# Layer 0: the dt transfers of the scan steps move from SP's queue to ACT's

## The chip, the core and the metric

The kernel runs on one core of a Trainium2 chip. A core has five engines with an instruction stream each: TensorE (PE, with its weight loads shown as PEld), VectorE (DVE), ScalarE (ACT), GpSimd (POOL) and SyncE (SP). Each engine works through its own stream in order, and streams meet at semaphores. Transfers between device memory and the on-chip memory are run by 16 DMA engines; an instruction on SP, ACT or POOL issues them into a queue of that engine. The metric is the device time of one execution in microseconds. Three executions of the kernel before took 7145.44, 7160.09 and 7180.47 us; the median is 7160.09 us.

## The reference

Four layers follow each other on x of 8 x 128 x 64 x 64, each of the form x + f(group_norm(x)). Layer 0 is a selective scan (a Mamba block) on the first 64 channels and a 3x3 convolution on the other 64; layer 1 passes over rows and columns in four directions, each row adding the relu of a 9-tap convolution of the row before; layer 2 is a product of two convolutions; layer 3 is a deformable convolution with a batch norm. The change lies in the scan of layer 0:

```python
dt = jax.nn.softplus(dbc[..., :R] @ dt_w + dt_b)      # per token, 128 channels
Bm = dbc[..., R:R + N]                                 # per token, N = 16
Cm = dbc[..., R + N:]
A = -jnp.exp(A_log)                                    # 128 channels x 16
dA = jnp.exp(dt[..., None] * A)
dBx = dt[..., None] * Bm[:, :, None, :] * xc[..., None]

def step(h, inp):
    dA_t, dBx_t, C_t = inp
    h = dA_t * h + dBx_t
    return (h, jnp.einsum('bdn,bn->bd', h, C_t))
```

For every image there are 128 x 16 recurrences of 4096 tokens.

## The kernel before, in words

**Tiling of the scan.** An image's 4096 tokens are cut into 4 chunks of 1024, so there are 32 chunks for 8 images; a chunk has two halves of T = 512 tokens. The 128 x 16 recurrences do not fit 128 partitions, so a half is worked off in 8 *steps*, each of 16 channels: a step has two tiles side by side (j = 0, 1), and in each, 8 channels times 16 states fill the 128 partitions. That gives 16 steps a chunk and 512 steps in all (`where`, L584).

**What one step needs.** The chunk's part of the program computes dt and u = dt * xc for 128 channels and stores both to device memory (`v_store`, L449, tiles dtd and ud). A step then reads 8 rows of them back, each repeated for the 16 states. This is `spread` (L590): for each j one transfer of 128 partitions x 512 floats, 256 KB, so two transfers for dt (k = 0) and two for u (k = 1). `step_dt` (L598) brings dt into a tile `da` (5 buffers); `step_u` (L602) brings u into a tile `hb` (6 buffers).

Then the step runs through the engines:

- `step_decay` (L606, ACT): da = exp(a * da) in place, two activations.
- `step_scan` (L612, DVE): ub = hb * B into PSUM (L619), and two hardware scans over 512 tokens (L627) that write the states back into hb. With the scan, da is free again.
- `step_carry` and `step_weigh` (L631, L635, POOL): the last states are kept for the next half; hb = hb * C.
- `round_sum` (L640, PE): for every two steps, four matmuls with a matrix of ones and zeros sum over the states into ps_y. With these, hb is free again.

**The order of the work.** Nothing is reordered by a scheduler: the loop at L659 writes the streams in a fixed order, and this order is the order on each engine and in each queue. Iteration i holds, in this order: step_scan(i); the vector instruction of layer 1 (`layer1.add`); step_dt(i + 4); round_sum(i - 3) if i is odd; step_u(i + 3); step_decay(i + 2); step_carry and step_weigh(i - 1); the events planned for iteration i; the matmuls of layer 1 (`layer1.products`). The events are the chunk's other work, planned by `plan_chunk` (L338) at fixed places relative to the chunk's first step: projections on PE and their evacuation by ACT (L368, L369, L402, L413, L428, L429, L461, L505, L516), Silu (L417) and Ln (`logs`, L300) with their table loads on ACT, the softplus sums on POOL, stores and loads on SP. The evacuated PSUM tiles (`ps_g`) share two buffers, so PE's next projection waits for ACT's evacuation of the one before the last.

**Layer 1 beside it.** From iteration 269 on, half of the images pass through layer 1 while layer 0 goes on: every iteration adds 9 matmuls (L763) and one vector instruction (L771). A new direction of layer 1 loads its weights (L752) on SP just ahead of its first matmuls.

**Transfers and their semaphores.** All transfers of layer 0 are issued by SP. Transfers that SP or ACT issue take eight completion semaphores in turn, in the order of the program, so an issue waits until the transfer eight places earlier has landed.

Of the kernel before, what the change touches and what calls it, by code (L numbers as in the profile page):

```python
# [22 lines left out]
GC, D, DI, N, R, KC = 64, 64, 128, 16, 4, 3  # L23
T = 512
# [140 lines left out]
def layer0(tc, a, ident, gmat, x_in, x1d, mid, norm1, layer1):  # L165
# [5 lines left out]
    nc = tc.nc  # L171
# [4 lines left out]
    with ExitStack() as ctx:  # L176
# [38 lines left out]
        with tc.manual_schedule():  # L215
# [368 lines left out]
            def where(i):  # L584

                return i // 16, i // 8 % 2, i // 2 % 4, 2 * (i % 2)
# [3 lines left out]
            def spread(i, k, t):  # L590

                c, h, r, j0 = where(i)
                for j in (0, 1):
                    d = 32 * (j0 + j) + 8 * r
                    src = dtu[c % 2][h][k][d : d + 8, :]
                    nc.sync.dma_start(t[:, j], src.unsqueeze(0).to_broadcast([N, 8, T]))

            def step_dt(i):  # L598
                steps[i] = {"da": w2.tile([P, 2, T], F32, name="da", bufs=5)}
                spread(i, 0, steps[i]["da"])  # L600

            def step_u(i):  # L602
                steps[i]["hb"] = w2.tile([P, 2, T], F32, name="hb", bufs=6)
                spread(i, 1, steps[i]["hb"])
# [810 lines left out]
```

## Time and profile before

| | |
|---|---|
| median of three runs | 7160.09 us (7145.44 to 7180.47) |
| profiled execution: time | 7110.95 us |
| profiled execution: span, first to last instruction | 7109.2 us |
| layer 0, first to last scan | 87.6 to about 2801 us |
| busy over the span: PE, DVE, ACT, POOL | 71%, 68%, 50%, 57% |
| da transfers on SP | 1024 of 256 KB |
| hb (u) transfers on SP | 1024 of 256 KB |
| moved over the whole span | 1496.93 MB, 211 GB/s on average |

The page gives busy time for each engine, and shares over slices of the span. In a line of a group, the first number after the bar is the busy time in us, then the mean of one instruction in ns, then the idle time of the engine before these instructions with what ended it. "L610 ACT ACTIVATE da<-da,a_neg" is line 610 on ACT, writing tile da from da and a_neg. An engine's name with a q (SPq, ACTq) is its sequencer: issues of transfers and waits, which are not busy time. In the views of waits a line reads: who waited, for whom, how long in total, how often, the longest. PEclk is the clock that TensorE was granted, DMA the mean busy share of the 16 DMA engines.

### The profile page before, as it was taken

What the parts mean: (1) busy time and instruction counts of PE and PEld (TensorE: products, weight loads), DVE (VectorE), ACT (ScalarE), POOL (GpSimd) and SP (SyncE); (2) the same over time, 40 slices, a digit from 0 to 9 for tenths busy, and PEclk for the clock granted to TensorE, in tenths of its full rate; (3) what the DMA queues carried; (4) which work ended last, traced back from release to release, by engine and by line L of the source; (5) the groups of instructions that cost most, each with busy time, mean ns of one, the idle gap of its engine ahead of it and who ended that gap; (6) DMA issues with size and microseconds to landing.
All of it is one profiled execution on the core that took longest, in us unless ns stands there. A gap on an engine that the chain in (4) does not pass through costs nothing. (4 is left out here: it accounts for less than half of the span.)

```text
span 7109.2 us, 74945 instructions
## 1 busy us (share of the span) xinstructions
PE 5077.6 (71%) x21034; PEld 3201.4 (45%) x21034; DVE 4815.8 (68%) x6350; ACT 3530.0 (50%) x8194; POOL 4037.7 (57%) x3739
## 2 busy tenths in 40 slices
PE   4666566799999999699987978975556565564331
PEld 1111111366666666477676766753333333333221
DVE  5988888777777766411466756768667676776667
ACT  4656656544444442200355545554556655655554
POOL 4877777665655554000355556566666666666661
PEclk7666666799999999899999989987767777687665
DMA  6999999988888876501366656677666666667668
GB/s 198 303 284 279 287 302 276 263 224 221 221 217 217 221 207 163 169 20 52 120 189 187 203 174 198 198 222 245 208 208 221 209 210 212 208 207 229 182 181 287
DMA packets 666176, 1496.93 MB, mean 211 GB/s; under 512 B 92712, under 2 KB 127792, under 8 KB 663712
## 3 DMA queue, kind: packets, MB, share of 16 engines
q1 hardware_dynamic: 475680, 871.24, 43.2%
q0 software_dynamic: 184320, 604.13, 27.9%
q10 hardware_dynamic: 5760, 16.78, 0.6%
q8 instruction: 168, 2.75, 0.2%
q14 instruction: 248, 2.03, 0.1%
HBM read 1337.03 MB, written 154.76 MB: 210 GB/s over the span
## 5 line engine op out<-in xcount | busy, mean ns | idle before, releaser
L1213 POOL DMA_INDIRECT X<-table,idx x1386 | 1318.5, 951 | 715.8 <-issue 273.4
L1213 POOL DMA_INDIRECT got<-table,idx x918 | 885.0, 964 | 1204.9 <-DVE idx L1103 508.5
L638 POOL TENSOR_TENSOR hb<-hb,C 128x1024 f32<-128x1024 f32 x512 | 1209.1, 2362 | 40.9
L627 DVE TENSOR_TENSOR_SCAN hb<-da,carry,ps_ub 128x512 f32<-128x512 f32 x896 | 1097.9, 1266 | 55.1 <-DVE ps_ub L619 0.5
L771 DVE SCALAR_TENSOR_TENSOR X<-ps_l,X 128x256 f32<-128x256 f32 x504 | 212.1, 421 | 1138.7 <-PE ps_l L763 954.5
L610 ACT ACTIVATE da<-da,a_neg 128x512 f32<-128x512 f32 x1024 | 695.2, 716 | 545.6 <-DMA da<-dtd 492.4
L1259 ACT COPY samp<-ps_s 128x384 f32<-128x384 f32 x768 | 362.5, 472 | 1039.4 <-remote 625.8
L1224 ACT ACTIVATE X<-X,wgt 128x128 f32<-128x128 f32 x2772 | 863.4, 396 | 9.8 <-issue 9.7
L1267 PE MATMUL ps_o<-samp,dcn_w 128*128 128x256 f32 x2304 | 706.6, 452 | 160.2 <-issue 119.7
L1249 PE MATMUL ps_s<-ident,X 128*128 128x128 f32 x1386 | 305.8, 343 | 595.6 <-ACT samp L1259 282.9
L619 DVE TENSOR_TENSOR ps_ub<-hb,ps_b 128x1024 f32<-128x1024 f32 x512 | 625.7, 1222 | 118.8 <-DMA hb<-ud 113.1
L1267 PEld LDWEIGHTS ps_o<-samp,dcn_w 128*128 128x128 f32 x2304 | 504.3, 230 | 282.6 <-issue 153.4
L646 PE MATMUL ps_y<-hb,m_y 128*32 128x512 f32 x2048 | 413.1, 758 | 269.1 <-DVE y L477 183.2
L1240 DVE TENSOR_TENSOR prod<-prod,X 128x384 f32<-128x384 f32 x462 | 260.9, 565 | 475.0 <-ACT X L1224 310.7
L633 POOL COPY carry<-hb 128x2 f32<-128x2 f32 x512 | 111.9, 219 | 826.6 <-DVE hb L627 789.2
L763 PE MATMUL ps_l<-X,w_left 128*128 128x256 f32 x2268 | 521.2, 386 | 80.6 <-DVE X L771 48.8
L763 PE MATMUL ps_l<-X,w_right 128*128 128x256 f32 x2268 | 524.9, 388 | 69.7 <-DVE X L771 58.3
L1224 ACT ACTIVATE got<-got,wgt 128x128 f32<-128x128 f32 x1836 | 570.4, 393 | 2.4 <-DMA got<-table,idx 2.4
L763 PE MATMUL ps_l<-X,w_up 128*128 128x256 f32 x2268 | 518.3, 384 | 48.3 <-DVE X L771 24.1
L763 PE MATMUL ps_l<-X,w_down 128*128 128x256 f32 x2268 | 516.6, 383 | 35.7 <-DVE X L771 27.3
L1249 PEld LDWEIGHTS ps_s<-ident,X 128*128 128x128 f32 x1386 | 206.1, 176 | 727.1 <-ACT samp L1259 357.6
L763 PEld LDWEIGHTS ps_l<-X,w_right 128*128 128x128 f32 x2268 | 438.7, 197 | 171.3 <-DVE X L771 83.7
(217 smaller groups left out, 8412.0 us busy)
## 6 DMA issues: line engine op xcount, KB each, us to landing
da<-dtd SPq DMA_DIRECT2D x1024, 256.0 KB
hb<-ud SPq DMA_DIRECT2D x1024, 256.0 KB
table<-tok SPq DMA_DIRECT2D x128, 256.0 KB
x<-x1d SPq DMA_DIRECT2D x96, 256.0 KB
X<-table,idx POOLq DMA_INDIRECT x1386
x<-x2d SPq DMA_DIRECT2D x48, 384.0 KB
x3h<-x3d SPq DMA_DIRECT2D x16, 1056.0 KB
x_st<-in_x SPq DMA_DIRECT2D x64, 256.0 KB
```

Source lines behind the costliest of these rows:

```text
L610: nc.scalar.activation(da[:, j], da[:, j], AF.Exp, scale=a_neg[:, r, j0 + j : j0 + j + 1])
L619: nc.vector.tensor_mul(ub, hb, s["B", h].unsqueeze(1).to_broadcast([P, 2, T]))
L627: nc.vector.tensor_tensor_scan(hb[:, j, :], st["da"][:, j, :], ub[:, j, :], start, ALU.mult, ALU.add)
L638: nc.gpsimd.tensor_mul(hb, hb, S[c]["C", h].unsqueeze(1).to_broadcast([P, 2, T]))
L646: nc.tensor.matmul(S[c]["ps_y", h][32 * j : 32 * j + 32, :], lhsT=m_y[:, r, :], rhs=steps[i + j // 2]["hb"][:, j % 2, :], start=(r == 0), ...
L763: nc.tensor.matmul(ps[:, c0:c1, :], lhsT=w[:, k, :], rhs=v[:, prev, c0 + k - PAD : c1 + k - PAD, :], start=(k == PAD), stop=(k == K - 1),)
L1213: nc.gpsimd.indirect_dma_start(out=got[:, k, :, :].rearrange("p q c -> p (q c)"), out_offset=None, in_=tab, in_offset=bass.IndirectOffsetO ...
L1224: nc.scalar.activation(got[:, k, q, :], got[:, k, q, :], AF.Identity, scale=wgt[:, t, k0 + k, q : q + 1])
L1240: nc.vector.tensor_add(prod[:, :, 0, :], prod[:, :, 0, :], got[:, :, 2, :])
L1249: nc.tensor.transpose(ps[:, k, :], got[:, k, 0, :], self.ident)
L1259: self.nc.scalar.copy(self.samp[k0][:, :, col : col + P], ps)
L1267: nc.tensor.matmul(ps, lhsT=self.dcn_w[:, k, :], rhs=samp[:, k - k0, :], start=(k == 0), stop=(k == KK - 1))
```

## The change

In `spread`, the transfers with k = 0 (dt) are issued by ACT instead of SP; those with k = 1 (u) stay on SP. The places of both in the program's order stay as they are, and so do tiles, buffers and sizes.

```diff
                 for j in (0, 1):
                     d = 32 * (j0 + j) + 8 * r
                     src = dtu[c % 2][h][k][d : d + 8, :]
-                    nc.sync.dma_start(t[:, j], src.unsqueeze(0).to_broadcast([N, 8, T]))
+                    queue = nc.sync if k else nc.scalar
+                    queue.dma_start(t[:, j], src.unsqueeze(0).to_broadcast([N, 8, T]))
```

In ACT's stream the two issues of step_dt(i + 4) stand right ahead of the two activations of step_decay(i + 2), behind the events of iteration i - 1. What the issues have to wait for (the buffer of da, the stored dt, the semaphore of the transfer eight places earlier) ACT now waits for, in its own stream. All later line numbers of the file grow by one.

## The prediction

> **What bounds the kernel now.** I read the slices of the page first, since the change touches only layer 0, which ends near 2815 us (its last scan starts at 2798.7 us). Slices are 178 us each; digits are tenths.
>
> ```profile
> PE   4666566799999999699987978975556565564331
> ...
> DVE  5988888777777766411466756768667676776667
> ACT  4656656544444442200355545554556655655554
> ...
> DMA  6999999988888876501366656677666666667668
> ```
>
> Two stages show. Up to about 1400 us DMA stands at 9 and PE at 5 to 7; from there to 2800 us PE stands at 9 and DMA at 7 to 8. In the second stage the matmuls of layer 1 (`products`) run beside the steps of layer 0. The busy time of the two stretches gives the figures.
>
> ```profile
> core 0: us, PE busy (x) PEld busy (x) DVE busy (x) ACT busy (x) POOL busy (x), PEclk, DMA share, GB/s
> 100.00:1360.00 1260.00, 808.02 (x2345) 192.30 (x2346) 1087.44 (x988) 754.83 (x1068) 960.99 (x742) 0.64 1.04 289
> 1440.00:2720.00 1280.00, 1210.53 (x5667) 807.65 (x5666) 933.74 (x967) 553.97 (x806) 752.47 (x585) 0.98 0.82 219
> ```
>
> First stretch: the 16 DMA engines have a share of 1.04 (packets overlap a little), DVE 86%, ACT 60%. From the packet records I counted half-microseconds: in 1.3% of this time the engines lack work. 268 steps pass, 4.7 us each. Second stretch: PE is busy 95% of the time and the engines lack work for a fifth of it; 212 steps, 6.0 us each; a chunk of 16 steps takes 92.4 us, nearly to the tenth, over and over. So the first half is bound by the DMA engines, the second by PE.
>
> Next, what SP itself waits for in its queue, first stretch and second (issuer, releaser: us, times, longest):
>
> ```profile
> SPq L596 <- DMA hb<-ud: 111.5, 272, 0.9
> SPq L596 <- DMA da<-dtd: 92.5, 256, 1.0
> SPq L596 <- PE ps_y L646: 73.8, 46, 5.5
> SPq L596 <- DVE hb L627: 44.3, 70, 2.3
> ```
>
> ```profile
> SPq L596 <- PE ps_y L646: 573.1, 106, 16.3
> ```
>
> The first two lines are the limit on transfers in flight: the program gives its transfers eight completion semaphores in turn, and an issue waits until the transfer eight places earlier has landed. The ps_y lines are u: its buffer hb comes free only after round_sum on PE, and the dt behind it in SP's queue waits too, 573 us in the second stretch.
>
> Last, ACT: a normal chunk in the second half, and an issue from ACT's own queue (only the end of the kernel has them).
>
> ```profile
> 1648.54 1.37 ACT L505 ACTIVATE res<-ps_c,conv_b 64x512 f32<-64x512 f32 x2 [12.09 <-PE ps_c L497]
> 1649.94 1.33 ACT L610 ACTIVATE da<-da,a_neg 128x512 f32<-128x512 f32 x2
> 1655.29 1.26 ACT L402 ACTIVATE xz<-ps_x,b_xc 128x512 f32<-128x512 f32 x2 [4.02 <-issue]
> 1656.45 1.33 ACT L610 ACTIVATE da<-da,a_neg 128x512 f32<-128x512 f32 x2
> 1661.25 1.26 ACT L413 ACTIVATE xz<-ps_z,in_b 128x512 f32<-128x512 f32 x2 [3.47 <-PE ps_z L411]
> ```
>
> ```profile
> 7030.06 1.24 ACT L1348 ACTIVATE X<-X,bn_shift,bn_sc 128x1024 f32<-128x1024 f32 x1 [1.78 <-DVE x3k L1352]
> 7030.14 0.37 ACTq L1353 DMA_DIRECT2D out<-x3k  x1
> 7031.20 1.23 ACT L1348 ACTIVATE X<-X,bn_shift,bn_sc 128x1024 f32<-128x1024 f32 x1
> ```
>
> ACT comes early to what PE makes for it (brackets: 12, 4 and 3.5 us of waiting), and an issue (0.37 us) runs while the activation before it is still computing.
>
> **The change, part by part.** *Issues.* 1024 transfers of 256 KB leave SP and come to ACT, two per step, just ahead of step_decay(i+2). The nearest row is their issue on SP:
>
> ```profile
> L596 SPq DMA_DIRECT2D da<-dtd x1024: 514/526/1790, 76.8 to 2773.7; - x171
> ```
>
> So 1.05 us a step. The issue in the end stage lay under the running activation, and a decay lasts 0.72 us; I let 0.5 us a step show: 0.5 x 512 = 256 us of ACT over the layer. ACT is idle 1260 - 755 = 505 us in the first stretch and 1280 - 554 = 726 us in the second, so it fits. If nothing were hidden it would be 1.05 x 268 = 281 us in the first, which fits too. On the path: 0.
>
> *Waits that come to ACT.* (a) da has five buffers, so dt(i+4) waits for step_scan(i-1) on DVE. Behind it on ACT stand decay(i+2) and all of that iteration's events (evacuations of PSUM, Silu, Ln); PE waits for those, DVE for the decay. Taken step by step from the trace, the scan ends after decay(i+2) starts today in 25% of the steps of the first half and 36% of the second, by 3.6 us at the 95th percentile. (b) The semaphore of eight transfers earlier: by the order of issue that is mostly dt(i+2), which ACT needs next anyway, or u(i+1); some are x_o, x1d or dtd transfers of SP. (c) At a chunk's start, dtd itself. With (a), (b) and the whole 1.05 us together, decay(i+2) would start 1.2 us later on average in the first half and 1.8 in the second; of its lead over the scan that uses it (median 9 and 13.6 us) at least 2.9 us is left at every step. In the second half (a) bites in iterations 10 to 15 of a chunk, ahead of the 12 us wait for ps_c, which swallows it; PE's Silu-fed matmul (L427) starts typically 7 us after Silu. On the path: 0. Between ends: if all of (a) and (b) got through once per chunk, 3.6 us x 32 chunks = +115; below nothing: none, as a wait added to ACT gives nothing back.
>
> *What SP sheds.* dt no longer stands behind u's wait for PE. Today SP issues dt(i+4) later than ACT reaches its place: by 0.9 us (median, first half) and 1.75 us (second). In the second half PE is the bound and decays lead by 9 us and more at 95 steps in 100, so the 573 us are not on the path: 0. In the first half the gain can only be the 1.3% in which the engines lack work: between 0 and -17 us; I take the middle, -8.
>
> *Weights of the next direction.* PE stood idle 9.5, 10.4 and 7.6 us at the three switches inside the layer, waiting for a 576 KB load on SP. It now shares the engines with dt from another queue instead of queueing behind it: half of 27.5 us either way, ±14; I take 0.
>
> *The rate of the engines.* dt and u would now reach the engines from two queues at once, which no row of layer 0 shows. Stretches of 72 us in the first half moved from 262 to 323 GB/s with the same kinds of transfer, so the order in which packets mix does move the rate. Ends: 1260 x (1 - 289/323) = -133 us, and 1260 x (289/262 - 1) = +130. The value taken is 0, as the mean over the stage is a mix already.
>
> A rule speaks against any gain here: the Trainium skill, "DMA: Bandwidth & Descriptors", section "Issuing engines are not separate DMA queues", says that transfers started by different engines run on the same 16 DMA engines and interleave, and that only issue time is saved. By the rule this term is 0; by the fastest stretch above it could be -133; issue time is no bound by SP's rows.
>
> **Sum.** 0 + 0 - 8 + 0 + 0 = -8 us. The profiled execution took 7110.95 us (span 7109.2 and 1.75 around it), 49.1 below the median of the runs, 7160.09. So 7103 in its terms, 7152 as a median.
>
> **The rivals.** *Faster by mixing.* Two queues break the march of 16 engines through the same rows. For it: 262 to 323 GB/s today, and a 2 KB packet took 117 ns on average in the first half, while stores at the same time took 84 to 91 ns. Against: b_in, C and plain loads are as slow, 115 to 130 ns, so the cause may lie elsewhere. Half of the 133: -67, with the -8: 7085.
>
> *Slower: the engines run dry behind ACT.* One mechanism: while ACT is held, no dt is issued. Its longest blocks are Silu (table 1.28, 1.91, table 1.28: 4.5 us) and the Ln group at 873.51 to 878.4 us (4.9), 9.4 us a chunk. If the engines stand still for half, 4.7 x 17 chunks of the first half = +80: 7240. It decides once dt is later than today by more than is in flight: transfers land about 5 us after issue in the first half (from the packet records). Against: ACT's place is 3.1 us behind SP's issue at the 95th percentile, and u still flows.
>
> *Slower by mixing.* The same unknown with the other sign, half of 130: +65, 7217.
>
> **How the numbers follow.** No real change 0.40; faster by mixing 0.33; engines dry 0.17; slower by mixing 0.10. Half a percent, 36 us, is about what this kernel's runs can tell (they span 7145 to 7180). So faster 0.33, same 0.40, slower 0.27. The likeliest case's own range is 7124 to 7196. Cases of both signs are likely, so the 80% range reaches 100 us below 7152, past the middle of the faster case, and 78 above, to where the dry case has begun to bite: 7052 to 7230.
>
> **What the profile after would show.** Right: 1024 da transfers in ACT's queue at about 0.52 us; DMA share still 1.0 and about 4.7 us a step up to 1400 us; 92.4 us a chunk afterwards; SP's ps_y wait still there, now holding u alone. Mixing: the first half's GB/s moves with the share still at 1.0. Dry: the share falls below 1 with ACT waiting for DVE or a landing. The forecast is wrong, too, if the 92.4 us grow, with PE waiting for an activation of ACT.

## The result and the profile after

Four executions of the changed kernel took 7272.43 to 7299.74 us, with a median of 7279.16; four of the kernel before had a median of 7152.76. The ratio is 1.0174, with a 95% interval of 1.0154 to 1.0194: 126 us slower. The profiled execution took 7272.43 us, its span 7270.7. The profiled execution of the kernel before, 7110.95 us, was 42 us under its median, this one 7 under: the two profiles lie 161 us apart, 35 of them behind layer 0, where nothing was changed.

The slices of the page tell where. Changed kernel, 182 us a slice, digits in tenths:

```profile
PE   4555565599998999699898978975556555565331
...
DVE  4778777777677777420376666758667676676667
ACT  4555555554444443210255555554556655555554
...
DMA  6999999988787878410266666667666666667667
```

The first half is lower on DVE and ACT; the digits of DMA hardly show it, since a 9 stands for 90% or more. The two stretches that the prediction used, for the changed kernel:

```profile
core 0: us, PE busy (x) PEld busy (x) DVE busy (x) ACT busy (x) POOL busy (x), PEclk, DMA share, GB/s
100.00:1360.00 1260.00, 722.73 (x2112) 168.68 (x2114) 989.18 (x891) 688.52 (x976) 856.36 (x671) 0.64 0.96 261
1440.00:2720.00 1280.00, 1195.25 (x5531) 788.18 (x5524) 939.72 (x977) 586.45 (x843) 754.79 (x587) 0.97 0.82 222
```

In the first stretch the DMA share fell from 1.04 to 0.96, 289 to 261 GB/s, and every engine does about 9% less work in the same time (DVE 1087 to 989 us, ACT 755 to 689). The second stretch is as it was. For sizes I use one measure throughout, read from the trace: the time from the ub product of step 8 to that of step 264, 256 steps of the first half, below called *the stage*. It took 1197.4 us before and 1321.9 after: +124.5, nearly all that layer 0 lost (126.7 from the first scan to the last). Steps 272 to 448 took 1063.2 and 1060.4, and the usual chunk of the second half takes 92.4 us in both. The loss has two parts. Counted in half-microseconds, the engines lacked work for 1.4% of the stage before and for 8.7% after (17 and 115 us, +98); and a 2 KB packet took 117.0 ns before, 119.1 after, 1.8% or some 20 us more. Each stage is of one profiled execution, so differences of some 10 us between runs carry no weight here.

The issues themselves came out as drawn. The row of ACT's queue for the tile da in the changed kernel, durations as minimum, median and maximum in ns:

```profile
L597 ACTq DMA_DIRECT2D da<-dtd x1024: 521/522/1671, 75.6 to 2899.4; - x171
```

What is new are waits. First ACT's, 100 to 1400 us, before and then after (who waited, for whom, us in total, times, longest):

```profile
ACT da L610 <- DMA da<-dtd: 238.8, 172, 4.4
ACT X L738 <- DMA x<-x1d: 111.7, 32, 8.7
ACT res L505 <- PE ps_c L497: 59.2, 14, 8.5
```

```profile
ACT da L611 <- DMA hb<-ud: 193.1, 61, 7.0
ACT da L611 <- DMA da<-dtd: 83.0, 30, 5.4
ACT da L611 <- DVE ps_ub L620: 67.5, 22, 6.2
ACT da L611 <- DVE hb L628: 54.9, 23, 4.6
```

Before, a decay waited for its own dt: ACT had come early. After, the same place waits for landings of u (193 us) and for DVE (67.5 and 54.9): that is what the issues ahead of the decay wait for, the semaphore of the transfer eight places earlier and the buffer of da. Counted from the records, the decays wait for their own operands only 6 us of the stage now; before it was 253 us. ACT has gone from early to late.

Then DVE's waits in the same time, before and after:

```profile
DVE ps_ub L619 <- DMA hb<-ud: 91.2, 71, 3.2
DVE gm L282 <- PE ps_gn L281: 37.5, 5, 9.0
```

```profile
DVE hb L628 <- ACT da L611: 61.8, 41, 4.5
DVE xz L435 <- ACT xz L432: 58.8, 12, 5.2
DVE gm L282 <- PE ps_gn L281: 51.8, 4, 14.1
DVE ps_ub L620 <- ACT ps_b L473: 37.6, 16, 4.4
DVE ps_ub L620 <- DMA hb<-ud: 20.9, 13, 2.8
```

Before, no wait of DVE for ACT stands above half a microsecond in total; after, there are three, 158 us: scans for decays, `v_round` (L435) for `v_exp` (L432), and the first ub product of a chunk for the copy of B into PSUM (L473). Against that DVE waits 70 us less for u. By position the loss lies there too: over 15 chunks of the first half, the mean time from one ub product to the next grew at steps 3 and 4 of a chunk (+0.9 and +1.2 us), 6 (+3.4), 14 and 15 (+1.3 and +3.2); at 1 and 2 it fell by 0.9 each; the rest is within 0.25. A chunk went from 74.6 to 82.5 us.

One held issue, in the timeline of ACT's stream in the changed kernel (start us, us, engine, line, what; in brackets the idle time before it and what ended it):

```profile
753.63 0.54 ACTq L597 DMA_DIRECT2D da<-dtd  x1
754.00 1.25 ACT L413 ACTIVATE xz<-ps_z,in_b 128x512 f32<-128x512 f32 x2
757.86 0.52 ACTq L597 DMA_DIRECT2D da<-dtd  x1
758.42 1.33 ACT L611 ACTIVATE da<-da,a_neg 128x512 f32<-128x512 f32 x2 [3.18 <-DMA hb<-ud]
762.27 1.18 ACTq L597 DMA_DIRECT2D da<-dtd  x2
763.50 0.72 ACT L611 ACTIVATE da<-da,a_neg 128x512 f32<-128x512 f32 x1 [3.74 <-DMA x_st<-in_x]
```

The first issue of a pair goes at 753.63, the second only at 757.86, when a u transfer has landed; the decay, whose data has long been there, starts 0.56 us later. The next pair is held until 762.27.

SP, which the change was to relieve, waits longer for PE than before: dt no longer stands ahead of u in its queue, and PE runs later behind ACT (from 100 to 1400 us its waits for ACT add up to 331 us, before to 133). SP's queue in the changed kernel, 100 to 1400 us, and then 1440 to 2720:

```profile
SPq L597 <- PE ps_y L647: 454.9, 91, 14.6
```

```profile
SPq L597 <- PE ps_y L647: 748.1, 105, 17.8
```

The first was 85 us before in the same time. The second was 573, and costs nothing: PE bounds that half.

### The profile page after: what moved, and what is told of

Read it like the earlier page. It is cut to its first block, busy times and chain, and to the rows that moved or that the text cites. A ratio compares the mean times of both kernels' runs of the same rounds, so it can differ in the third digit from the quotient of the medians.

```text
span 7270.7 us, 74786 instructions
## 1 busy us (share of the span) xinstructions
PE 5090.7 (70%) x21034; PEld 3209.2 (44%) x21034; DVE 4824.2 (66%) x6350; ACT 3534.6 (49%) x8194; POOL 4017.8 (55%) x3739
## 4 chain that ended last, share of the span: by engine, by line
PE 29%; ACT 11%; another core or an unknown queue 7%; issue 6%; DVE 5%; DMA 2%; POOL 0%; SPq 0%; ACTq 0%; DVEq 0%; POOLq 0%
PE ps_l L764 13%; ACT X L1225 6%; PE ps_o L1268 5%; PE ps_t L926 4%; PE ps_s L1250 3%; PE ps_off L1043 2%; PE ps_t L952 2%; ACT samp L1260 1%; ACT got L1225 1%; DVE prod L1230 1%; DVE X L772 1%; DVE prod L1241 0%; DMA x<-x1d 0%; DVE got L1242 0%
## 5 line engine op out<-in xcount | busy, mean ns | idle before, releaser
L764 PE MATMUL ps_l<-X,w_up 128*128 128x256 f32 x2268 | 517.3, 384 | 54.9 <-DVE X L772 34.5
L764 PEld LDWEIGHTS ps_l<-X,w_left 128*128 128x128 f32 x2268 | 439.9, 198 | 182.1 <-DVE X L772 81.6
```

Source lines behind the costliest of these rows:

```text
L764: nc.tensor.matmul(ps[:, c0:c1, :], lhsT=w[:, k, :], rhs=v[:, prev, c0 + k - PAD : c1 + k - PAD, :], start=(k == PAD), stop=(k == K - 1),)
```

## The experiments

Three theories stood at the start. **The loop** (where an expectation uses letters: L, and L2 in the form through PE): ACT and SP hold each other through the completion semaphores and through u's wait for PE. **Mixing**: two queues make the engines themselves slower. **ACT is full**: issue time, holds and the tie to DVE's scan use up ACT's idle time, so that all that ACT makes comes late. (In the expectations I is the issue time alone, B the tie alone; L3, that a held ACT holds back the next dt.) Layer 0 takes about the same time on the chips used (the stage of the controls h3 and j2: 1203 and 1213 us), but on those of the last seven runs the later layers are faster (the kernel before takes some 6660 us there), so the stage, not the whole time, is compared between calls. Each ratio is against the kernel before on its own chip.

| run | what is on ACT | ratio, 95% interval | stage us | engines lack work |
|---|---|---|---|---|
| before | - | 1 | 1197.4 | 1.4% |
| after | dt | 1.0174 [1.0154, 1.0194] | 1321.9 | 8.7% |
| e1_u_one_act | dt; u as one transfer | 1.0290 [1.0273, 1.0308] | 1398.8 | 9.5% |
| e2_u_one_sp | control: u as one | 1.0150 [1.0131, 1.0169] | 1290.3 | 4.0% |
| e3_act_busy | issue time alone | 1.0014 [1.0003, 1.0024] | 1212.8 | 1.9% |
| e4_act_tie | tie alone | 1.0028 [1.0013, 1.0043] | 1225.8 | 1.8% |
| f1_act_lane | hold alone | 1.0012 [0.9995, 1.0029] | 1201.5 | 2.0% |
| f2_u_later_act | dt; u one iteration later | 1.0200 [1.0174, 1.0226] | 1343.5 | 8.1% |
| f3_u_later_sp | control: u later | 1.0040 [1.0026, 1.0054] | 1243.7 | 3.2% |
| f4_u_on_act | u, with dt on SP | 1.0281 [1.0256, 1.0306] | 1352.9 | 8.3% |
| g1_act_hold | hold and tie | 1.0068 [1.0047, 1.0089] | 1245.2 | 3.2% |
| g2_free_act | dt; u free of PE | 1.0178 [1.0154, 1.0203] | 1340.5 | 8.4% |
| g3_free_sp | control: u free of PE | 0.9944 [0.9926, 0.9963] | 1169.5 | 1.3% |
| h1_act_all | issue time, hold and tie | 1.0141 [1.0109, 1.0173] | 1290.7 | 4.7% |
| h2_short_act | dt; decays cut short | 1.0055 [1.0038, 1.0073] | 1247.0 | 3.0% |
| h3_short_sp | control: decays cut short | 0.9989 [0.9973, 1.0005] | 1203.3 | 1.0% |
| h4_half_act | half of dt | 1.0065 [1.0038, 1.0091] | 1240.3 | 2.2% |
| i1_later_act | dt, behind the decays | 1.0211 [1.0193, 1.0228] | 1338.5 | 7.8% |
| j1_round_act | dt; v_round later | 1.0182 [1.0165, 1.0199] | 1316.3 | 7.6% |
| j2_round_sp | control: v_round later | 1.0027 [1.0012, 1.0043] | 1212.6 | 1.8% |

### Fewer transfers per step, and the burdens one by one

u as one transfer of 512 KB (the two rows of a pair lie side by side in ud, so its store is changed too), with dt on ACT and on SP; a cut of the edit:

```diff
 ...
+                if k:
+                    src = dtu[c % 2][h][k][8 * r : 8 * r + 8, j0 : j0 + 2, :].rearrange("q a t -> q (a t)")
+                    queue.dma_start(t.rearrange("p a t -> p (a t)"), src.unsqueeze(0).to_broadcast([N, 8, 2 * T]))
+                    return
 ...
```

> dt stays on ACT in two issues a step; u becomes one transfer of 512 KB on SP (rows of a pair stored side by side), so that a step takes three completion semaphores of the eight instead of four and the transfer eight places earlier is an older one. Theory L (ACT is held at its issues by the semaphore of the transfer eight places earlier): most of the hold goes, steps 8 to 264 take 1190 to 1250 us instead of 1322, within 40 us of the same kernel with dt on SP. Theory I (the time of the issues on ACT) and theory B (the wait for scan(i-1) on ACT): nothing changes for them, 1300 to 1340 us and 100 to 140 us behind the same kernel with dt on SP.

> The control of the one above: u as one transfer, dt back on SP. All theories: the first half stays bound by the DMA engines, steps 8 to 264 take 1140 to 1210 us (before: 1197); packets of 4 KB may make it somewhat shorter.

Measured: 1398.8 against 1290.3, so dt on ACT costs 108 us with three semaphores a step in place of four. The loop expected at most 40; that failed, and 108 lies in the 100 to 140 of the others. The stages themselves are longer than any expectation, since the control is itself 1.5% slower than the kernel before, where 1140 to 1210 us was expected.

The two other runs leave all transfers on SP and give ACT one burden each at the place of the dt issues: three activations of 128x128 on a scratch tile (issue time), or a write of one column into da(i-1), which waits for the scan of step i-1 and which SP's dt must then wait for (the tie).

```diff
+                    for _ in range(3):
+                        nc.scalar.activation(spare, spare, AF.Identity)
                     step_dt(i + 4)
```

> The kernel before (dt on SP), with three activations of 128x128 on a scratch tile put on ACT where step_dt stands, about 0.9 us of ACT time a step and no wait. Theory I: about the loss of the change, +90 to +130 us. Theories L and B: ACT is idle 40% of the first half, so 0 to +25 us.

```diff
+                    if i >= 1:
+                        nc.scalar.activation(steps[i - 1]["da"][:, 0, 0:1], eps, AF.Identity)
                     step_dt(i + 4)
```

> The kernel before (dt on SP), with an activation of one column into the buffer of da(i-1) put on ACT where step_dt stands: ACT waits there for scan(i-1), and SP's dt(i+4) for that place of ACT, but no issue and no semaphore of another transfer stands on ACT. Theory B: +90 to +130 us. Theories L and I: 0 to +35 us.

Measured: +15 and +28 us of the stage. ACT was busy 76% of the stage in e3 and still had 100 us of decays that came early. Neither alone makes 125.

### The hold, the loop through u, and u on ACT

f1 lets ACT wait, at the same place, for the landing of u(i+1), and do nothing else. f2 and f3 bring u one iteration later, so that it waits less for PE. f4 puts u on ACT and leaves dt on SP. The edits of f1, of f2 and f3, and of f4:

```diff
+                    if i >= 0:
+                        nc.scalar.activation(spare, steps[i + 1]["hb"][:, 1, T - 1 : T], AF.Identity)
                     step_dt(i + 4)
```

> The kernel before (dt and u on SP), with one activation on ACT where step_dt stands that reads one column of hb(i+1) after its transfer: ACT waits for the landing of u(i+1), as the semaphore of the transfer eight places earlier makes it in the changed kernel, but no issue stands on ACT and there is one queue. Theory L2 (a loop: ACT waits for u to land, SP issues u late because it waits for round_sum on PE, and PE waits for ACT's evacuations and Silu): +50 to +130 us, with PE waiting for ACT much longer than before. If this wait is not the cause: 0 to +25 us.

```diff
-                if 0 <= i + 3 < n_steps:
-                    step_u(i + 3)
+                if 0 <= i + 2 < n_steps:
+                    step_u(i + 2)
```

> The changed kernel (dt on ACT) with u issued one step later in the program, step_u(i+2) instead of step_u(i+3): SP then asks for a buffer of hb that PE freed an iteration earlier, so its wait for ps_y shrinks, and the transfer eight places before dt is an older u. Theory L2: most of the loss is gone, within 50 us of the same with dt on SP. If the loss came from issue time, from the wait for scan(i-1) or from mixing two queues: still 90 to 140 us behind the same with dt on SP.

> The control of the one above: the kernel before with step_u(i+2) instead of step_u(i+3). All theories: the first half stays bound by the DMA engines; -20 to +40 us, the plus if u now lands late for DVE.

```diff
-                    queue = nc.sync if k else nc.scalar
+                    queue = nc.scalar if k else nc.sync
```

> The mirror of the change: u on ACT, dt on SP. ACT now waits for round_sum on PE itself. Theory L2: the loop is closed without a detour and the loss is larger than the change's, +150 to +400 us, in the second half too. Issue time alone or two queues alone: as in the change, +100 to +140 us, in the first half only.

The hold alone costs 4 us, although ACT stands there for 295 us of 1300. The waits of ACT in f1:

```profile
ACT spare L666 <- DMA hb<-ud: 294.9, 147, 5.6
ACT X L741 <- DMA x<-x1d: 100.1, 32, 6.4
```

It took the place of the 239 us that the decays had waited for dt. f2 less f3 is still 100 us: a second miss for the loop. (f3 itself is 46 us longer than the kernel before, a little more than expected.) f4 is worse than the change: its stage is 156 us longer than before, and it is the one run that clearly slowed the second half (steps 272 to 448: 1096.4 us against 1063.2). That is what the loop had expected for it (+150 to +400 us, the second half too); but u on ACT brings PE's wait to ACT directly, and what it says of dt on ACT the next runs decide.

### Hold and tie together, and u free of PE

g1 joins the hold and the tie: one column of hb(i+1) is written into da(i-1). In g2 and g3, `round_sum` reads a constant tile in place of hb, so u's buffer no longer waits for PE; with dt on ACT and on SP. These two leave out the sum over the states, with as many matmuls of the same size. Of their edit only the operand is shown.

```diff
+                    if i >= 1:
+                        nc.scalar.activation(steps[i - 1]["da"][:, 0, 0:1], steps[i + 1]["hb"][:, 1, T - 1 : T], AF.Identity)
                     step_dt(i + 4)
```

> dt and u on SP; on ACT, where step_dt stands, one activation of one column that reads hb(i+1) and writes into the buffer of da(i-1). So ACT is held there for the landing of u(i+1) and for scan(i-1), and dt(i+4) cannot be issued before ACT has passed: hold and tie together, with neither the issues on ACT nor a second queue. Theory L3 (what costs is that a held ACT holds back the next dt, so that the engines run out of work; neither the hold nor the tie alone does it, they cost 7 and 24 us): +70 to +150 us, engines idle 5 to 10% of steps 8 to 264. If the issues themselves or the two queues are needed: the sum of the two parts, +15 to +45 us.

```diff
 ...
-                        rhs=steps[i + j // 2]["hb"][:, j % 2, :],
+                        rhs=in_w.unsqueeze(1).to_broadcast([P, 2, 2 * DI]),
```

> The changed kernel (dt on ACT), but round_sum's matmuls read a constant weight tile instead of hb (the sum over the states is left out, so layer 0's scan output is not the reference's; the same number and size of matmuls). hb comes free after POOL, and SP's u no longer waits for PE. Theory L3 with the loop through SP (ACT held for a u that SP issues late because of PE): the loss against the same kernel with dt on SP falls below 50 us. If SP's lateness is no part of it: 90 to 140 us as before.

> The control of the one above, with the same part left out (round_sum reads a constant weight tile) and dt on SP. The first half stays bound by the DMA engines: -25 to +10 us against the kernel before; the 570 us of SP's wait for ps_y in the second half go.

g1 cost 48 us: just above the sum of the parts (15 to 45), below the 70 to 150 expected if holding back dt were all. With u free of PE the change costs more, 1340.5 - 1169.5 = 171 us, above both expectations. The first stretch of g2, then of g3 (columns as above):

```profile
100.00:1360.00 1260.00, 735.07 (x2080) 171.05 (x2082) 972.53 (x878) 670.23 (x955) 845.10 (x662) 0.58 0.96 258
```

```profile
100.00:1360.00 1260.00, 826.64 (x2486) 215.13 (x2487) 1108.75 (x1011) 770.16 (x1090) 974.25 (x753) 0.62 1.04 295
```

With dt on SP the engines use the freedom (295 GB/s), with dt on ACT they do not (258, share 0.96). SP's wait for PE, 455 us in the changed kernel, is therefore a consequence, and the loop through PE is out.

### All burdens on ACT without a transfer, and less work on ACT

h1 puts hold, tie and issue time on ACT and leaves every transfer on SP. h2 does the reverse: dt on ACT, but the decays compute 4 of 512 columns, and what `v_store` stores as dt is the logarithm's result, so that the factors stay below one; h3 is its control. Both leave out most of the decay. h4 moves only the second of the two transfers of dt.

```diff
+                    if i >= 1:
+                        nc.scalar.activation(steps[i - 1]["da"][:, 0, 0:1], steps[i + 1]["hb"][:, 1, T - 1 : T], AF.Identity)
+                    for _ in range(3):
+                        nc.scalar.activation(spare, spare, AF.Identity)
                     step_dt(i + 4)
```

> dt and u both on SP as in the kernel before. At the place of the dt issues ACT gets all three things that those brought to it, without any transfer: an activation of one column that waits for the landing of u(i+1) and for the scan of step i-1 (it writes a column of da(i-1), so that SP's dt(i+4) waits for it), and behind it three activations of 128x128 as issue time. Theory 'ACT is full' (issue time, hold and tie add up on one engine that works in order, more than each alone because together they leave it no idle time): steps 8 to 264 at 1300 to 1340 us against 1197, ratio 1.014 to 1.020. Theory 'two issuers' (the order of landing matters: eight completion semaphores go round over two queues, and each issuer waits for transfers of the other): no more than the parts measured one by one, +15 for the time and +48 for hold and tie, so 1250 to 1275 us, ratio 1.007 to 1.011.

```diff
-                    for k, t in enumerate((s["rv"], s["w"])):
+                    for k, t in enumerate((s["e"], s["w"])):
 ...
-                    nc.scalar.activation(da[:, j], da[:, j], AF.Exp, scale=a_neg[:, r, j0 + j : j0 + j + 1])
+                    nc.scalar.activation(da[:, j, :4], da[:, j, :4], AF.Exp, scale=a_neg[:, r, j0 + j : j0 + j + 1])
```

> dt on ACT, as in the changed kernel, but ACT has less to do: the decay exponential computes 4 of the 512 columns of each tile (the rest of da stays dt), and dtd holds the logarithm's result instead of dt, so that the factors stay below one. All waits stay: ACT still waits for dt's landing before the short decay, the scan still waits for ACT. About 1 us a step leaves ACT, more than the 0.7 us of issue time that shows in the changed kernel. Theory 'ACT is full': the loss goes with the load; less than 40 us in steps 8 to 264 above the control with dt on SP, ratio of the two below 1.006. Theory 'two issuers': the loss stays, 90 us or more above the control, ratio of the two 1.012 or more.

> The control of the run with the short decay: the same 4 columns and the same stored logarithm, with dt on SP as in the kernel before. Both theories: within 1% of the kernel before, 1180 to 1210 us in steps 8 to 264, since the DMA engines bound this stage and they move the same bytes.

```diff
-                    queue = nc.sync if k else nc.scalar
+                    queue = nc.scalar if j and not k else nc.sync
```

> Of the two transfers of dt per step, the first stays on SP and the second is issued by ACT. Theory 'ACT is full': one issue a step, half the time and fewer places at which ACT is held; about half of the loss, +40 to +75 us in steps 8 to 264 (1237 to 1272 us), ratio 1.006 to 1.011. Theory 'two issuers': the semaphores still go round over two queues, and the loss is nearly whole, +90 us or more, ratio 1.012 or more.

h1: 1290.7 us, +93, between the two expectations (1250 to 1275 and 1300 to 1340), its ratio 1.0141 inside that of "ACT is full". The parts one by one had cost 15 and 48: together they cost more than their sum, and three quarters of the change's loss in time came without a second queue. But it is not the same loss. The engines lacked work for 60 us, 44 more than before, where the change has 98 more; the other half of h1's loss is packets of 122.0 ns (118.0 in h3, on the same chip), slower than those of the changed kernel, from one queue. The first stretch of h1, and DVE's waits, 100 to 1400 us:

```profile
100.00:1360.00 1260.00, 774.57 (x2154) 179.85 (x2156) 1020.60 (x914) 918.63 (x1998) 881.44 (x690) 0.63 1.00 267
```

```profile
DVE ps_ub L619 <- DMA hb<-ud: 102.0, 94, 3.1
...
DVE hb L627 <- ACT da L667: 38.7, 31, 2.5
DVE xz L435 <- ACT xz L432: 20.7, 12, 1.8
...
DVE ps_ub L619 <- ACT ps_b L473: 1.3, 2, 0.7
```

DVE waits 61 us for ACT here, 158 in the changed kernel. So h1 shows that burdens on ACT alone make ACT late and the engines run dry, at less than half of the size.

h2 less h3 is 1247.0 - 1203.3 = 44 us, though ACT is held at the issues even longer than in the changed kernel (395 us of the stage against 345): with 0.84 us a step less to compute (503 against 719 us busy) it carries most of the holds. The expectation was under 40 for "ACT is full", 90 or more for two issuers; 44 is near the first. The engines lack work for 25 us more than in h3, not 98: most of this part goes with ACT's work, though both issues stay on ACT. DVE waits 46 us for ACT, h2, 100 to 1400 us:

```profile
DVE xz L435 <- ACT xz L432: 36.5, 13, 3.4
...
DVE ps_ub L620 <- ACT ps_b L473: 5.2, 4, 2.3
DVE hb L628 <- ACT da L611: 4.3, 12, 1.8
```

h4 cost 43 us, 10 of them by lack of work: a third of the whole, at the lower end of "about half" (40 to 75) and far from the 90 of two issuers.

Where ACT's time goes bears on why the burdens do not add. All counted from the records of the stage, in us; "shown issue" is issue time in which no activation ran on ACT, "held" the wait ahead of an issue or of the operation put in its place, "early" all other waits, in which ACT stood ready before its operands (gaps under 0.06 us are left out); "lost" and the two columns behind it are against the kernel before: of the stage, of the time in which the engines lack work, and of what the packets took of the 16 engines' time.

| run | stage | busy | shown issue | held | early | lost | by lack of work | by slower packets |
|---|---|---|---|---|---|---|---|---|
| before | 1197 | 720 | 0 | 0 | 472 | 0 | 0 | 0 |
| e4_act_tie | 1226 | 747 | 0 | 88 | 385 | 28 | 5 | 25 |
| e3_act_busy | 1213 | 918 | 0 | 0 | 274 | 15 | 6 | 10 |
| f1_act_lane | 1202 | 732 | 0 | 279 | 186 | 4 | 7 | -5 |
| h4_half_act | 1240 | 709 | 90 | 249 | 181 | 43 | 10 | 35 |
| g1_act_hold | 1245 | 733 | 0 | 359 | 149 | 48 | 22 | 21 |
| h2_short_act | 1247 | 503 | 205 | 395 | 126 | 50 | 20 | 29 |
| i1_later_act | 1339 | 713 | 162 | 334 | 119 | 141 | 88 | 51 |
| h1_act_all | 1291 | 938 | 0 | 222 | 110 | 93 | 44 | 49 |
| after | 1322 | 719 | 171 | 345 | 70 | 125 | 98 | 19 |

The last two do not add up exactly, as transfers also overlap. The early time is the cover. It was 472 us; issue time and holds of 516 us need more than that, and by the bottom line 70 is left, mostly at waits for what PE makes. While 180 or more were left, a burden cost no more than 10 us by lack of work; at 126 to 149 it cost some 20, at 110 and 70 it cost 44 and 98. One row, i1, does not fit (the next section): 119 left and 88 lost, 64 of the 119 at decays. That the cover is what runs out is thus read from these rows and from h2, not isolated by one run.

The packets' part follows no such order. It is there with one queue (e4, g1, h1) as with two, and what makes a packet slower was not found.

### By which way it reaches DVE

In the changed kernel the decay of step i+2 stands right behind the issues. i1 puts the issues behind it. j1 takes away DVE's largest single wait for ACT: `v_round` goes one iteration later; j2 is the control.

```diff
-                if 0 <= i + 4 < n_steps:
-                    step_dt(i + 4)
 ...
                 if 0 <= i + 2 < n_steps:
                     step_decay(i + 2)
+                if 0 <= i + 4 < n_steps:
+                    step_dt(i + 4)
```

> dt on ACT as in the changed kernel, but issued behind the decays of step i+2 instead of ahead of them. Theory 'ACT is full': the same time and the same holds stand in ACT's stream, only one place later, ahead of the evacuations and Silu instead of the decay; the loss stays between 80 and 150 us in steps 8 to 264 (1280 to 1350 us), ratio 1.011 to 1.020. Rival 'the decay stands behind the hold': the loss comes because decay(i+2), and with it the scan, waits behind the issues; then it falls below 50 us (under 1247 us), ratio under 1.007.

```diff
-                at(t0 - 10, v_round)
+                at(t0 - 9, v_round)
```

> dt on ACT as in the changed kernel; v_round, the one DVE instruction that reads v_exp's result, goes one iteration later in DVE's stream (iteration 16c-9 instead of 16c-10), behind one more scan. Theory 'DVE stands at three places of a chunk where it needs something of a late ACT' (v_round for v_exp 58.8 us, the first ps_ub of a chunk for the copy of B 37.6 us, scans for decays 61.8 us, in 1300 us of the first half): the first of them shrinks to under 20 us and steps 8 to 264 fall by 25 to 60 us against the changed kernel, to 1260 to 1297 us; ratio against the kernel before 1.008 to 1.014. Rival 'it only moves' (ACT stays as late and the DMA engines as dry, so DVE waits for the next decay or copy instead): steps 8 to 264 above 1305 us, ratio 1.015 or more, with the wait for v_exp gone and those for decays or the copy longer.

> The control: v_round one iteration later, dt on SP as in the kernel before. There DVE has no wait for v_exp, so both theories: no difference, steps 8 to 264 at 1187 to 1207 us, ratio 0.997 to 1.003.

i1 lost 141 us, no less than the change and inside the 80 to 150 of "ACT is full": the decay's place is not it. What moved is the position: step 14 of a chunk is whole again (+0.04 us), and step 15 is 5.6 us longer. By the program's order the hold ahead of the next chunk's dt now stands between decay(14) and decay(15), and DVE waits longer for the copy of B, i1, 100 to 1400 us:

```profile
DVE ps_ub L620 <- ACT ps_b L473: 73.2, 16, 6.2
DVE xz L435 <- ACT xz L432: 58.0, 12, 5.1
...
DVE hb L628 <- ACT da L611: 31.7, 29, 3.2
```

j1 went against my expectation for the theory that DVE's three places are the path (1260 to 1297 us): 1316.3, the rival's "it only moves". The wait for v_exp is gone, and the others took over its time, j1:

```profile
DVE hb L628 <- ACT da L611: 92.2, 68, 5.2
DVE ps_ub L620 <- ACT ps_b L473: 73.7, 27, 5.7
```

61.8 + 58.8 + 37.6 = 158 us in the changed kernel, 92.2 + 73.7 = 166 here. So the places where DVE waits are where the lateness of ACT is paid; removing one did not make ACT earlier. j2 was 15 us slower than the kernel before in the stage, a little outside what was expected.

What stays open: of the 98 us in which the engines lack work, burdens without a transfer (h1) bring back 44. For the rest, that two issuers hold each other by the eight semaphores is possible; no run isolates it, nor did a run give da a sixth buffer, with which an issue would wait for an older scan. The packets' part is not explained at all. No version that computes the whole result beats the kernel before.

## Why the prediction was wrong

The forecast was 7152 us, range 7052 to 7230; the time is 7279. By its own steps:

- **What bounds the kernel, and the second half: right.** The second half did not move (steps 272 to 448: 1063.2 and 1060.4 us), nor did the wait of SP for PE of 748 us cost anything. All depended on the first half. That a chunk there takes 92.4 us over and over holds for half of them; most others take 94 to 112, before and after.
- **Issues.** I let 0.5 us a step show; 171 us over 256 steps are 0.67. Their own price, "on the path: 0", is nearly right: the same time alone costs 15 us (e3).
- **Waits that come to ACT: this step failed.** It put them at 0, at most +115 if all of (a) and (b) got through once per chunk. The working took the times of the old trace as fixed and found decays 1.2 us later on average, with 2.9 us left at every step. Measured from the start of a decay to the scan that uses it, the median lead in the stage fell from 8.9 to 3.2 us, by 5.7 and not 1.2. (The 3.6 us at the 95th percentile in (a) are the second half's; the first half's are 2.7.) The holds and the shown issues take 516 us, 2.0 a step. How 1.2 grew to 5.7 I can only argue: a late decay makes a late scan, that a late buffer of da and a later issue; no run cuts this circle alone. Two waits were not followed at all: `v_round` behind `v_exp`, and the ub product behind the copy of B. They are 96 of the 158 us that DVE came to wait for ACT. And the sum "505 us idle, so it fits" weighed issue time alone against ACT's idle time; with the holds that time is used up, and the holds and issues share one cover. Alone, hold, issue time and tie cost 7, 6 and 5 us by lack of work (f1, e3, e4), together 44 (h1).
- **What SP sheds: no gain.** The -8 was for engines that lack work, and they lack it for 98 us more. The bound taken from that 1.3% (17 us) does not hold either as a price of u's wait: with u free of PE and dt on SP, the stage is 28 us shorter (g3), by faster packets (114.1 ns).
- **Weights of the next direction: right.** PE's waits for them at the three switches are 9.7, 11.6 and 6.9 us after, 28.2 in all against 27.5.
- **The rate of the engines: small, but not 0.** 0 taken, +1.8% measured for a 2 KB packet, some 20 us. The Trainium skill's page "DMA: Bandwidth & Descriptors", section "Issuing engines are not separate DMA queues", says that transfers of different issuers share the engines and that only issue time is saved. The trace agrees in so far as two queues brought no more: 261 against 289 GB/s in the first stretch, 119.1 against 117.0 ns. The section speaks of what can be saved, not of what can be lost; here the loss came with 345 us of holds.
- **The rivals.** "The engines run dry behind ACT" is what happened, with a chance of 0.17, and its sign in the profile was right: share 0.96, ACT waiting for landings and DVE. Its size (+80) and its place were not: it counted Silu and Ln, 4.7 us a chunk, in which no dt is issued. The loss is 7.9 us a chunk, at steps 3, 4, 6, 14 and 15, and ACT's issues are held for 345 us of the stage. "Slower by mixing" had the sign but not the size: 1.8% against an end of 10%; and packets as slow or slower came from one queue as well (h1, 122.0 ns), so that mixing is the cause is not shown. "Faster by mixing" did not happen.

## What to carry to other kernels

Issuing a transfer from a compute engine gives that engine's in-order stream the transfer's waits (buffer, source, completion semaphore); price the holds and the issue time together against the idle time in which the engine is early, stage by stage, not each alone against its idle total. Do not replay the old trace with fixed times where the engine's products free the buffers that its issues wait for. The burden can be tried without the change, by one small instruction that reads what the transfer would wait for, and a few that take its time; here that brought back the sign and 93 of 125 us, but only 44 of the 98 us in which the engines lacked work. A time alone does not tell that: split the loss into engines without work and slower packets.

## What the runs showed that was not expected

- One transfer of 512 KB with 4 KB packets is slower than two of 256 KB with 2 KB: 246 ns a packet on SP against 2 x 119 for the 2 KB packets beside it (e2), and the stage 93 us longer with fewer issues: 34 us by lack of work, 35 by packet time, and less overlap.
- ACT can stand still for 295 us of 1300 and the kernel loses 4 us in the stage (f1), while three burdens that cost 4 to 28 us alone, or 48 for two of them, cost 93 together, half of it by slower packets though all transfers stay in one queue.
- Taking PE's read of hb away made 2 KB packets faster, 117.0 to 114.1 ns (g3); what links them was not looked into.
